# Modulation matmuls spread in twos over two stretches of a factorization, and a third token tile kept in SBUF

## The chip, the cores and the metric

The kernel runs on one NeuronCore of a Trainium2 chip. The metric is the device time of one launch in microseconds (us); lower is better. The engines that matter here are TensorE (PE, with its weight loads shown as PEld), VectorE (DVE), ScalarE (ACT), GpSimd (POOL) and SyncE (SP), which here only issues DMAs.

## The reference

The input `x` has 8 batches of 512 tokens of width 576, and `cond` one row of 576 per batch. Everything is float32.

```
# L0: a rotation in a 64-dimensional subspace
U, _ = qr(P)                                  # P: 576 x 64
A    = skew(silu(cond) @ W.T + b)             # 8 matrices of 64 x 64
R    = expm(A)
x    = x + ((x @ U) @ R - x @ U) @ U.T

# L1: a transformer block with modulation
shift1, scale1, gate1, shift2, scale2, gate2 = split(silu(cond) @ ada_w + ada_b, 6)
h = layernorm(x) * (1 + scale1) + shift1
q, k, v = h @ qkv_w + qkv_b                   # 16 heads of width 36
att = softmax(q . k over the 16 heads of the same token) @ v
x = x + gate1 * (att reshaped @ proj_w + proj_b)
h = layernorm(x) * (1 + scale2) + shift2
x = x + gate2 * (gelu(h @ fc1_w + fc1_b) @ fc2_w + fc2_b)
```

The attention is over the 16 heads of one token, so it is elementwise work and runs on DVE, one tile of 128 tokens at a time.

## The kernel before

**Preparation.** The kernel factors `P` first, column by column, in a loop of 64 steps (`qr_step(j, ...)`, L259). A step has two matmuls, `rp` (L262, it broadcasts the pivot row) and `dp` (L270, it sums the column products), two small activations on ACT (`nrm` L286 and `nsg` L287) and about 20 DVE instructions. They wait for each other in a ring. `rp` needs the updated `m` of the step before (L325). `dp` needs the column products `t` (L251 and L256), which DVE makes after that update. DVE's first instruction of a step (`sg`, L279) needs `rp`, and its `w` (L308) needs `nrm`, which needs `dp`. The steps get shorter as the columns that remain get fewer.

**Work beside the factorization.** TensorE has free time in each step, and the generator `beside()` (L508) fills it. After the instructions of step `j`, for `j` above 1, the loop calls `next(side, None)` once, and the generator issues one portion. In the order of the steps the portions are:

- steps 4 to 13: four matmuls of `skew_entries` each (L385), which make the entries of the skew matrices;
- steps 14 to 17: modulation, that is `modulations()` (L497). It has 9 groups of 384 columns. A group is five matmuls of 8 x 384 (`ada`, L352, one for each block of 128 rows of `ada_w`), and a copy of the sums to `ada_rows` on ACT (L354). After groups 1, 2, 5 and 7 comes one more unit, `modulation(v)`: five matmuls of 8 columns (`mod`, L363) and two activations on ACT (L369 or L371). Each matmul of `ada` and each `modulation` is one unit of the generator, 49 units in all. A group whose buffer is free again loads another (`load_ada`);
- steps 18 to 30: the series of `expm` (L425), with products of 64 x 64 matrices (L409) on TensorE, copies on ACT and sums on POOL. Where the series yields `True`, which it does in 12 of these 13 steps, a portion of the modulation is issued too;
- steps 31 to 49: the 19 squarings of `expm` (`pe` and `pf`, L409), without modulation;
- from step 50: what is left of the modulation.

A portion of the modulation is three units: `paced(3, [modulations()])` (L513) yields after every third. After the 12 units of steps 14 to 17 and 36 units of the series, one unit is left for step 50. When the last `ada` matmul is done, the SBUF of the preparation is given to the weights of the main part, so SP's loads that follow (L1004, L902, L970) wait for it.

All engines but SP run the instructions here in the order in which they are recorded (`tc.manual_schedule`).

**The first tiles.** After the factorization the kernel solves for the projection and begins the main part (L1106 on). A unit is one pair of token tiles of 128. `qkv(b, i)` (L787) multiplies one tile by `wqkv` in six groups of 288 columns (`qkvp`, L800), each summed in one of two PSUM buffers (`ps_mm`). ACT copies a group out. For the first two tiles of batch 0 (`stay`, L791) the copy goes straight to `tok`, one of three SBUF buffers with the tag `qkv` (L808). For any other tile the copy goes to `qs` (L811), ACT issues a DMA of it to `tok_d` in DRAM (L812), and `attention` loads the whole tile back later with a DMA from SP (L826). The attention of a unit reads it on DVE (L838, L845, L866, L873).

Between the pieces of attention of unit 0 the hand-written order places the rotations of batches 0 and 1 (`zps` L730, `rot` L741, the sum and the normalization L749 and L137 to L141, with one power on POOL, L140), the transposes `htr` (L773), and `next_sums` (L996): on POOL four tensor operations (L1007 to L1010) on weights of fc2, and the DMA of their result to `comb_d` (L1000).

The DMAs of all queues share eight completion semaphores in turn. A DMA is only issued when the DMA recorded eight places before it, on the same semaphore, has landed. A queue stands still while it waits for that.

**The main part.** From about 410 us the 16 units follow each other: projection, MLP on TensorE, and the attention of the unit after next beside it on DVE. It is the same before and after.

Of the kernel before, what the change touches and what calls it, by code (L numbers as in the profile page):

```python
# [48 lines left out]
def rotate_then_dit_block(  # L49
# [53 lines left out]
    def srows(c):  # L103
        return 65 if c == 4 else 128
# [47 lines left out]
    with tc.manual_schedule(engines=engines), tc.tile_pool(name="prep", bufs=1) as prep, tc.tile_pool(name="qrs", bufs=2) as qrs, tc.tile_pool(  # L152
# [177 lines left out]
        def paced(n, parts):  # L330

            k = 0
            for part in parts:
                for _ in part:
                    k += 1
                    if k % n == 0:
                        yield
# [6 lines left out]
        def load_ada(g):  # L344
            aws[g] = adap.tile([128, NK, AC], F32, tag="aw", name=f"aw_{g}")
            load_rows(aws[g], ada_w[:, g * AC : (g + 1) * AC], 65)

        def ada_columns(g):
            ps = ps_m.tile([B, AC], F32, tag="m", name=f"ada_{g}")
            for c in range(NK):  # L350
                k = srows(c)
                nc.tensor.matmul(ps, lhsT=sc[0:k, c, :], rhs=aws[g][0:k, c, :], start=c == 0, stop=c == NK - 1)  # L352
                yield
            nc.scalar.copy(ada_rows[:, g * AC : (g + 1) * AC], ps)  # L354
            for k in range(2):
                if g == (4, 8)[k]:
                    nc.sync.dma_start(out=gates_d[k], in_=ada_rows[:, (3 * k + 2) * D : (3 * k + 3) * D])

        def modulation(v):
            ps = ps_m.tile([128, NK, B], F32, tag="m", name=f"mod_{v}")  # L360
            for c, rows in enumerate(KROWS):
                first = v * D + c * 128
                nc.tensor.matmul(  # L363
                    ps[0:rows, c], lhsT=ada_rows[:, first : first + rows], rhs=ident[0:B, 0:B], start=True, stop=True
                )
            for c0, c1, rows in ((0, 4, 128), (4, 5, 64)):
                dst = mod[0:rows, v // 3 * 2 + v % 3, c0:c1, :]
                if v % 3:
                    nc.scalar.activation(dst, ps[0:rows, c0:c1], AF.Identity, bias=ones[0:rows, 0:1])  # L369
                else:  # L370
                    nc.scalar.copy(dst, ps[0:rows, c0:c1])  # L371
# [7 lines left out]
        def skew_entries(g):  # L379

            ps = ps_m.tile([B, GROUP], F32, tag="m", name=f"skew_{g}")
            cols = slice(g * GROUP, (g + 1) * GROUP)
            for c in range(NK):
                k = srows(c)
                nc.tensor.matmul(ps, lhsT=sc[0:k, c, :], rhs=wr[0:k, c, cols], start=c == 0, stop=c == NK - 1)  # L385
                yield
            nc.scalar.mul(skew[:, 1 + g * GROUP : 1 + (g + 1) * GROUP], ps, 2.0**-N_SQUARINGS)
# [3 lines left out]
        def skew_rows():  # L391

            nc.sync.dma_start(out=skew_d, in_=skew)
            for h in range(2):
                for k in range(2):
                    first = skew_d[h * 4 : h * 4 + 4, k * 32 : k * 32 + R]
                    src = bass.AP(tensor=first.tensor, offset=first.offset, ap=[[62, 32], [VD, 4], [1, R]])
                    nc.sync.dma_start(out=au[h * R + k * 32 : h * R + k * 32 + 32], in_=src)
# [98 lines left out]
        def modulations():  # L497

            for g in range(9):
                yield from ada_columns(g)  # L500
                if g + 4 < 9:
                    load_ada(g + 4)
                v = {1: 0, 2: 1, 5: 3, 7: 4}.get(g)
                if v is not None:
                    modulation(v)
                    yield

        def beside():  # L508
            yield
            yield  # L510
            yield from paced(4, [skew_entries(g) for g in range(8)])
            skew_rows()
            rest = paced(3, [modulations()])  # L513
            for _ in range(4):
                next(rest)
                yield
            for free in expm(*eyes):
                if free:
                    next(rest, None)
                yield  # L520
            for _ in rest:
                yield

        for g in range(4):
# [6 lines left out]
        first_xt = xin.tile([128, D], F32, tag="xt", name="xt_0_0", bufs=2)  # L531
        eyes = identities()
        side = beside()
        t, done = column_products(0), None
        for j in range(R):
# [251 lines left out]
    def qkv(b, i):  # L787


        hT = hTs[b]  # L790
        stay = b == 0 and i < 2  # L791
        if stay:
            tok = toks[b, i] = tiles.tile([128, 3 * D], F32, tag="qkv", name=f"qkv_{b}_{i}", bufs=3)

        def group(n):
            cols = slice(n * HALF, (n + 1) * HALF)
            ps = ps_mm.tile([128, HALF], F32, tag="mm", name=f"qkvp_{b}_{i}_{n}")
            for c in range(NK):
                k = srows(c)
                nc.tensor.matmul(  # L800
                    ps,
                    lhsT=hT[0:k, c, i * 128 : (i + 1) * 128],
                    rhs=wqkv[0:k, c, cols],
                    start=c == 0,
                    stop=c == NK - 1,
                )
            if stay:
                nc.scalar.copy(tok[:, cols], ps)  # L808
            else:
                qs = tiles.tile([128, HALF], F32, tag="qs", name=f"qs_{b}_{i}_{n}", bufs=4)  # L810
                nc.scalar.copy(qs, ps)  # L811
                nc.scalar.dma_start(out=tok_d[b][i * 128 : (i + 1) * 128, cols], in_=qs)  # L812

        return [lambda n=n: group(n) for n in range(6)]
# [294 lines left out]
    first[0]()  # L1109
    feature_major(0, 0)  # L1110
    q = qkv(0, 0)
    now(q[:2])
    first[2]()
    now(q[2:4])
    first[3]()
    next_sums()
    now(q[4:])
    q = qkv(0, 1)
    att = attention(*units[0])
    ops(4, att)  # L1120
# [6 lines left out]
    next_sums()  # L1127
    feature_major(0, 1)
    now(qkv(0, 2))
    ops(4, att)  # L1130
    next_sums()
# [129 lines left out]
```

## Time and profile before

| | |
|---|---|
| median of 3 runs | 2169.66 us (2166.77 to 2171.46) |
| profiled execution, its own time | 2173.5 us |
| its span, first to last instruction | 2171.8 us |
| PE busy in the span | 2074.7 us (96%) |
| DVE busy | 1825.2 us (84%) |
| ACT, POOL busy | 401.4 us (18%), 658.7 us (30%) |
| mean granted TensorE clock | 0.964 |

The profiled execution took 3.8 us longer than the median. Its span leaves out 1.7 us of its own time. Busy time is the union of the engine's instructions. The granted clock is the share of its full speed that TensorE was allowed; in this trace it is either 1.0 or 0.5 at any moment.

By stage, in the same trace, PE was busy for 157.7 of the 170 us from 240 to 410, and for 1634.1 of the 1650 us from 410 to 2060.

### The profile page before, as it was taken

The page shows a single profiled execution, that of the slowest core. Times are in us where ns is not written, and L with a number is a line of the kernel's source. Part 1 is how long each engine was busy: PE and PEld are TensorE (multiplying, and loading weights), DVE is VectorE, ACT ScalarE, POOL GpSimd, SP SyncE. Part 2 cuts the span into 40 slices and gives each one's busy share as a digit, 9 for nine tenths or more (in the row PEclk, how much of TensorE's full clock was granted, in tenths as well). Part 3 has the DMA queues.
Part 4 walks back from the last instruction along what each step waited for, and adds up shares of the span by engine and source line. Part 5 has one row for each costly group of instructions (what it writes and reads, how often), then busy time and mean ns, then how long its engine had stood idle before and what let it go on. Part 6 is the DMA issues. An engine that isn't in the chain of part 4 may idle for free.

```text
span 2171.8 us, 27934 instructions
## 1 busy us (share of the span) xinstructions
PE 2074.7 (96%) x10087; PEld 1676.4 (77%) x10087; DVE 1825.2 (84%) x2544; ACT 401.4 (18%) x896; POOL 658.7 (30%) x918
## 2 busy tenths in 40 slices
PE   5896998999999999999999999999999999999988
PEld 3475666887878788888878787878888887787867
DVE  8998499799997979879797979797997999996930
ACT  2232121212121211111121212121111111112110
POOL 2341143242323232323232232323232323233322
PEclk9955799999999999999999999999999999999999
DMA  8202265484939476665758494847666676676754
GB/s 276 87 2 75 85 213 160 135 238 156 271 125 266 158 229 200 191 197 185 237 146 269 126 276 129 267 157 229 198 176 229 196 223 181 193 207 198 220 154 123
DMA packets 239789, 400.79 MB, mean 185 GB/s; under 512 B 85502, under 2 KB 127435, under 8 KB 239652
## 3 DMA queue, kind: packets, MB, share of 16 engines
q1 hardware_dynamic: 213732, 372.46, 56.3%
q10 hardware_dynamic: 25920, 26.55, 3.6%
q8 instruction: 80, 1.31, 0.3%
q14 instruction: 57, 0.47, 0.1%
HBM read 340.01 MB, written 58.94 MB: 184 GB/s over the span
## 4 chain that ended last, share of the span: by engine, by line
PE 58%; DVE 24%; issue 10%; POOL 4%; DMA 2%; ACT 1%; ACTq 0%; SPq 0%; POOLq 0%; DVEq 0%
PE fc L973 24%; PE fc L1044 8%; PE fc L1049 5%; PE qkvp L800 5%; DVE sc L845 4%; DVE att L873 4%; DVE qk L838 3%; PE fc L1046 3%; DVE pv L866 3%; PE pj L928 2%; PE p L1059 2%; PE zps L730 1%; PE rot L741 1%; PE dp L270 1%; DVE m L325 1%
## 5 line engine op out<-in xcount | busy, mean ns | idle before, releaser
L973 PE MATMUL fc<-h2T,w 128*128 128x256 f32 (+1 forms) x2880 | 653.6, 381 | 2.3 <-ACT h2T L949 1.5
L973 PEld LDWEIGHTS fc<-h2T,w 128*128 128x128 f32 (+1 forms) x2880 | 539.8, 191 | 79.7 <-ACT h2T L949 8.8
L800 PE MATMUL qkvp<-wqkv,hT 128*128 128x288 f32 (+1 forms) x1920 | 485.0, 410 | 8.0 <-ACT qs L811 5.8
L800 PEld LDWEIGHTS qkvp<-wqkv,hT 128*128 128x128 f32 (+1 forms) x1920 | 364.2, 192 | 110.3 <-ACT qs L811 7.6
L838 DVE TENSOR_TENSOR qk<-qkv 128x2304 f32<-128x2304 f32 x128 | 336.7, 2630 | 18.8 <-DMA qkv<-tok 15.0
L866 DVE TENSOR_TENSOR pv<-sc,qkv 128x2304 f32<-128x2304 f32 x128 | 333.1, 2602 | 2.8
L873 DVE TENSOR_REDUCE att<-pv 128x144 f32<-128x2304 f32 x128 | 326.1, 2548 | 2.6
L845 DVE TENSOR_REDUCE sc<-qk 128x64 f32<-128x2304 f32 x128 | 326.2, 2549 | 2.4
L1029 POOL TENSOR_TENSOR ss<-gt 128x128 f32<-128x128 f32 x144 | 109.9, 763 | 643.9 <-ACT gt L981 643.9
L981 ACT ACTIVATE gt<-fc 128x512 f32<-128x512 f32 x144 | 86.0, 597 | 769.2 <-PE fc L973 739.9
L1049 PEld LDWEIGHTS fc<-wt,ss 128*128 128x128 f32 x1152 | 160.6, 190 | 15.1
L1049 PE MATMUL fc<-wt,ss 128*128 128x144 f32 x1152 | 164.7, 286 | 0.0
L1044 PE MATMUL fc<-wq,gt 128*128 128x288 f32 x576 | 163.2, 405 | 0.0
L811 ACT COPY qs<-qkvp 128x288 f32<-128x288 f32 x180 | 71.7, 398 | 412.1 <-PE qkvp L800 356.1
L989 POOL TENSOR_TENSOR x<-x,mt 128x288 f32<-128x288 f32 x64 | 71.1, 1111 | 211.5 <-DVE mt L988 211.5
L1044 PEld LDWEIGHTS fc<-wq,gt 128*128 128x128 f32 x576 | 107.6, 189 | 22.6
L1032 POOL TENSOR_TENSOR s<-gt 128x128 f32<-128x128 f32 x144 | 108.3, 752 | 0.0
L140 POOL TENSOR_TENSOR rstd_m<-rstd_m,mhalf 128x1 f32<-128x1 f32 x32 | 21.2, 663 | 279.3 <-DVE rstd_m L139 244.5
L928 PE MATMUL pj<-w2q_p,aT 128*128 128x288 f32 x384 | 104.8, 408 | 0.5 <-DVE u L1079 0.5
L1046 PE MATMUL fc<-wq,ss 128*128 128x288 f32 x288 | 93.9, 408 | 2.8 <-POOL ss L1031 2.6
L1044 PE MATMUL fc<-wt,gt 128*128 128x288 f32 x288 | 93.4, 406 | 0.0
L831 DVE COPY sc<-s 128x1 f32<-128x1 f32 x14 | 2.1, 153 | 104.0 <-POOL s L1032 104.0
(254 smaller groups left out, 2290.6 us busy)
## 6 DMA issues: line engine op xcount, KB each, us to landing
w<-in_fc_w SPq DMA_DIRECT2D x288, 320.0 KB
wq<-in_fc_q SPq DMA_DIRECT2D x144, 432.0 KB
wt<-comb_d SPq DMA_DIRECT2D x144, 432.0 KB
tok<-qs ACTq DMA_DIRECT2D x180, 144.0 KB
qkv<-tok SPq DMA_DIRECT2D x30, 864.0 KB
w2q_p<-in_proj_w SPq DMA_DIRECT2D x32, 432.0 KB
xT<-in_x_t SPq DMA_DIRECT2D x16, 640.0 KB
xt<-in_x SPq DMA_DIRECT2D x32, 288.0 KB
```

The costliest lines, as they stand in the source:

```text
L800: nc.tensor.matmul(ps, lhsT=hT[0:k, c, i * 128 : (i + 1) * 128], rhs=wqkv[0:k, c, cols], start=c == 0, stop=c == NK - 1,)
L838: nc.vector.tensor_tensor(pr, q[:, c * HC : (c + 1) * HC].unsqueeze(2).to_broadcast([128, HC, H, DH]), k.unsqueeze(1).to_broadcast([128, H ...
L845: nc.vector.tensor_reduce(sc[t][:, c * HC : (c + 1) * HC, :], pr, AX.X, ALU.add)
L866: nc.vector.tensor_tensor(pr, sc[t][:, c * HC : (c + 1) * HC, :].unsqueeze(2).to_broadcast([128, HC, DH, H]), v.unsqueeze(1).to_broadcast( ...
L873: nc.vector.tensor_reduce(att[:, c * HC : (c + 1) * HC, :], pr, AX.X, ALU.add)
L928: nc.tensor.matmul(ps, lhsT=aT[0:k, c, :], rhs=w, start=c == 0, stop=c == NK - 1)
L973: nc.tensor.matmul(ps[:, k], lhsT=w1[0:n, c, :], rhs=h2T[0:n, c, 0 : NU * 128], start=c == 0, stop=c == NK - 1,)
L1029: nc.gpsimd.tensor_tensor(ss[:, 0], gt[:, 0, 1], gt[:, 1, 1], ALU.add)
L1032: nc.gpsimd.tensor_tensor(s3s[g], gt[:, 0, 0], gt[:, 0, 1], ALU.subtract)
L1044: nc.tensor.matmul(p[k], lhsT=whole[k][0], rhs=whole[k][1], start=g == 0, stop=stop)
L1046: nc.tensor.matmul(p[2], lhsT=whole[2][0], rhs=whole[2][1], start=g == 0, stop=stop)
L1049: nc.tensor.matmul(bank[:, side], lhsT=lhs, rhs=rhs[:, n * QUARTER : (n + 1) * QUARTER], start=False, stop=stop, skip_group_check=True,)
```

## The change

There are two edits, in two stages that are far from each other.

The first is in `beside()`. The modulation is no longer paced in threes. `some(n)` takes `n` units of it. Steps 14 to 17 still take three each. The 12 steps of the series that issue modulation take two each, so that 24 units are issued there where there were 36. The 13 units that are left, where there was one, follow in steps 50 to 56: two in each, and one in step 56. The `modulation` unit after group 7 is among them, in step 53. The number of instructions is the same.

The second is in `qkv`: `stay` holds for `i < 3`. The third tile of batch 0 is copied straight to the third `qkv` buffer. Six DMAs that ACT issued (144 KB each) and one that SP issued (864 KB) are gone.

```diff
@@ beside()
             skew_rows()
-            rest = paced(3, [modulations()])
+            rest = modulations()
+
+            def some(n):
+                return [next(rest, ended) for _ in range(n)][-1] is not ended
+
+            ended = object()
             for _ in range(4):
-                next(rest)
+                some(3)
                 yield
             for free in expm(*eyes):
                 if free:
-                    next(rest, None)
+                    some(2)
                 yield
-            for _ in rest:
+            while some(2):
                 yield
@@ qkv(b, i)
         hT = hTs[b]
-        stay = b == 0 and i < 2
+        stay = b == 0 and i < 3
         if stay:
             tok = toks[b, i] = tiles.tile([128, 3 * D], F32, tag="qkv", name=f"qkv_{b}_{i}", bufs=3)
```

The order of the instructions on DVE and POOL is the same in both kernels. On PE only the modulation's matmuls move, within steps 18 to 56. On ACT the copies and activations of the modulation move with them, and six DMA issues go. On SP one load goes, and the last loads and stores of the modulation come with the units that they belong to.

## The prediction

> **What bounds the kernel now.** I read the page first, then the windows by stage, the waits of DVE, and the timelines of PE and ACT around the edits.
>
> ```profile
> span 2171.8 us, 27934 instructions
> PE 2074.7 (96%) x10087; PEld 1676.4 (77%) x10087; DVE 1825.2 (84%) x2544; ACT 401.4 (18%) x896; POOL 658.7 (30%) x918
> ```
>
> The page says PE, but that is the main part, which the change does not touch. Both edits lie ahead of 410 us, where stages follow each other without overlap: a microsecond saved or lost there arrives whole at the end. Up to 210 us the ring of the factorization sets the pace, so I ask what DVE waits for.
>
> ```profile
> DVE sg L279 <- PE rp L262: 3.1, 5, 1.1
> DVE w L308 <- ACT nrm L286: 0.9, 3, 0.3
> ...
> DVE w L308 <- ACT nrm L286: 2.5, 12, 0.2
> ```
>
> The first two lines are the waits of 50 to 125 us, the last of 175 to 210 us. Beside the series DVE stands still 3.1 us because `rp` came late, five times. DVE is busy otherwise, so this is nearly all that thinner portions can give there. In the last steps it loses 0.2 us a step to `nrm`.
>
> ```profile
> core 0: us, PE busy (x) PEld busy (x) DVE busy (x) ACT busy (x) POOL busy (x), PEclk, DMA share, GB/s
> 62.90:66.31 3.41, 2.88 (x12) 1.19 (x12) 3.28 (x21) 0.44 (x2) 0.00 (x0) 1.00 0.95 287
> 66.31:69.72 3.41, 3.31 (x18) 1.80 (x18) 3.36 (x18) 1.15 (x5) 0.72 (x1) 1.00 0.33 80
> 69.72:73.14 3.42, 3.32 (x7) 1.14 (x8) 3.08 (x20) 0.44 (x2) 0.00 (x0) 0.50 0.48 180
> 120.92:124.34 3.42, 1.87 (x36) 1.61 (x36) 3.33 (x18) 0.92 (x4) 1.03 (x2) 1.00 0.00 0
> 175.54:178.95 3.41, 3.36 (x15) 1.79 (x12) 3.14 (x19) 1.28 (x4) 0.61 (x1) 0.50 0.00 0
> ```
>
> The clock (PEclk) changes at the edges of windows of 3.41 us. A window of three `ada` a step (62.90) keeps it full. One with two `ada` and a `mod` (66.31) halves the next, though PE was busy 3.31 of 3.41 us. A window full of `ada` at half clock (69.72) restores it. So streamed columns count, not busy time, and two `ada` a step lie close to the edge.
>
> ```profile
> 63.31 2.10 PE L352 MATMUL ada<-aw,sc 128*8 128x384 f32 x6
> 70.38 3.45 PE L352 MATMUL ada<-aw,sc 128*8 128x384 f32 x6
> ...
> 176.70 1.45 PE L352 MATMUL ada<-aw,sc 65*8 65x384 f32 x2
> 178.15 0.60 PE L262 MATMUL rp<-m,ident 128*128 128x13 f32 x2
> 178.80 0.57 PE L270 MATMUL dp<-t,ones 128*128 128x13 f32 x2
> 180.69 0.60 PE L262 MATMUL rp<-m,ident 128*128 128x12 f32 x2 [1.32 <-DVE m L325]
> ```
>
> Three `ada` (six instructions) take 2.10 us at full clock, 0.70 each; at half clock 3.45, 1.15 each. In step 51 PE is free for 1.32 us, at half clock. One unit fits there, two do not.
>
> **Part 1a, steps 18 to 30: 12 units less.** With two units the late `rp` should go: after step 18 (3.45 us becomes 2.30, and DVE waited 0.6), 19, 28 (3.74 becomes 2.5; it waited 1.1), 29 and 30: −3.1 us. Against it, at full clock a step of two streams less, about as the window from 66.31 did, so the clock will halve more often. The trace has four half windows between 69 and 124 us (from 69.72, 97.03, 107.27 and 114.10). I expect one to three more. In one, a step with 64 x 64 products and two `ada` needs about 1.2 for `rp` and `dp`, 1.1 for products and 2.3, together 4.6 us, against some 3.5 us of DVE; half of that excess is hidden, since `rp` may come as late as DVE's `sg`. At some 0.45 us each, two windows give +0.9. Bounds: −4.0 (both waits, 3.1 and 0.9, gone) and +0.5 (eight such windows). I take −2.2, nearer the gain, because the five waits are rows of the trace and the extra windows are an estimate.
>
> The Trainium skill, "TensorE: Matmul & The Clock Gate", Part 1, says that the clock falls after an idle window of about 3.4 us and that gaps shorter than this keep it up. By that rule no step of twos would ever halve it, and 1a would be the whole −4.0. The row from 66.31 speaks against the rule: no idle gap, and the next window halved. I go by the row.
>
> **Part 1b, steps 50 to 56: 12 units more.** All of this lies on the ring. The clock is at half from 124.34 on, since squarings do not lift it. From `rp` to the portion is 1.00 us (175.70 to 176.70), so step 50 takes 1.00 + 2.4 = 3.4 us against 2.45: +0.9. A window of such steps is as full of `ada` as that from 69.72, so the clock should rise within step 51: +0.4. At full clock `rp`, `dp` and two units take 0.57 + 1.40 = 1.97 us, under DVE's 2.25, and the wait for `nrm` goes: −0.2 for step 52. Step 53 holds `ada`, the wait for ACT's copy (0.24 in the trace) and `mod` (1.26): 0.57 + 0.70 + 0.24 + 1.26 = 2.8 against 2.5 us, with its activations +0.4. As after 66.31 the next window is halved: +0.8 in steps 54 and 55. Steps 56 to 58 at full clock: −0.5. Sum +1.8. Bounds: −1.8 (full clock throughout, 0.25 us for each of 7 steps) and +6.9 (half clock throughout: five steps at +0.95, and step 53 at 4.6 against 2.5). The 175.54 row, with a single `ada`, stayed at half; two is where I count on the rise.
>
> ACT's copies (0.47 us) lie between two `nrm` as before. SP's loads for the main part, issued from 178.22 to 184.5 after the last `ada`, move about 15 us later. DMA is at 259 GB/s just after 178.95 and at 25 GB/s in 200 to 240, and their first user is `next_sums` behind 240: nothing. Were that cover gone, SP would be late by as much as the loads overlap 240 us, at most a few.
>
> **Part 2, the third tile.**
>
> ```profile
> 284.64 0.34 ACTq L812 DMA_DIRECT2D tok<-qs  x1
> 285.69 0.40 ACT L811 COPY qs<-qkvp 128x288 f32<-128x288 f32 x1 [1.47 <-PE qkvp L800]
> 290.06 0.34 ACTq L812 DMA_DIRECT2D tok<-qs  x1
> 290.44 0.40 ACT L811 COPY qs<-qkvp 128x288 f32<-128x288 f32 x1 [4.36 <-DMA comb_d<-tt]
> ...
> 290.89 5.12 PE L800 MATMUL qkvp<-wqkv,hT 128*128 128x288 f32 x20 [0.39 <-ACT qs L811]
> ```
>
> ACT's second store waits 4 us for a semaphore that a `comb_d` store holds, and the next copy behind it. But PE had two PSUM buffers and lost 0.39 us. That goes. The load back was issued at 298.73; the `xT` load queued behind it waits for PE's `zps` (done at 299.7) anyway, and DVE reads the tile first at 367.99, long after. From 250 to 365 us DVE is the bound; it idles 1.48 us for `rot` at 300.97, which comes earlier by the same 0.39 us. Stores recorded later get other neighbours on the eight semaphores, only for eight of them. The later stalls (ACT at 340 to 363 us) hang on POOL's `next_sums` and on DVE and stay. Bounds: −1.9 (0.39 and all of the 1.48) and +0.3 (a neighbour that lands late). I take −0.6.
>
> **Sum:** −2.2 + 1.8 − 0.6 = −1.0 us. The profiled execution of 2173.5 would be 2172.5; it lies 3.8 us above the median, so the median becomes 2169.66 − 1.0 = 2168.7 us. A difference under 0.2% (4.3 us) is about what a measurement of this kernel can't tell from none.
>
> **Rivals.**
> - *PE is never late.* The twos fit, the clock rises at once in step 50 and holds. Early −4.0, late −0.3, tile −0.6: −4.9 us, 2164.8 us. For it: the five waits are real, and 1.97 is under 2.25 us. Against: the 66.31 row.
> - *The round trip was on the path.* The chain of waits lists the stores and the load (2.1 and 4.4 us) between PE and POOL's power. If true, −6.5 us on its own: 2163.2 us. Against: that power (L140) reads only what DVE's L139 wrote, which ended at the same moment.
> - *Half clock in the last steps.* If two units a step don't lift the clock, 1b is +6.9; with −1.0 early and −0.6: +5.3 us, 2175.0 us. It decides if steps 50 to 55 take over 3.2 us each. For it: the clock stayed at half through 40 us of squarings with PE busy throughout, and in the 175.54 row. Against: the rise after 69.72.
>
> The change does what it says: the instruction order shows the units in steps 50 to 56 and seven DMAs less.
>
> **How the numbers follow.** Forecast 0.50, PE never late 0.22, round trip 0.08, half clock 0.20. Faster by over 0.2%: 0.30; same 0.50; slower 0.20. The range reaches from 2163.8 to 2174.0: it takes in the first rival and most of the bounds, and leaves out the two ends. The forecast's own range is 2165.4 to 2172.0.
>
> **What would show it.** `rp` waits of DVE in 50 to 125 us near zero, more half windows there; step 31 begins some 2 us earlier (before 118.67). Steps 50 and 54 over 3 us, 52 under 2.4 us, PEclk 1.00 in a window between 178 and 192 us. No 4 us stall of ACT near 286 us, and `rot` of the second batch 2 us earlier or less. Wrong, if steps 51 and 52 stay over 3.2 us, or if DVE's wait for `rp` stays at 3 us.

## The result, and the profile after

The changed kernel took 2176.61 us (median of 9 runs, 2173.73 to 2182.49) where the kernel before took 2171.70 us (median of 9 runs, 2166.77 to 2173.99). The ratio is 1.0029, with a 95% interval from 1.0017 to 1.0040. The forecast was 2168.7 us with a range up to 2174.0, so it was wrong, and on the slow side.

One comparison was not the whole of it. The same two kernels were compared twice more, with ratios 0.9998 [0.9984, 1.0011] and 1.0031 [1.0021, 1.0041]. Together the 30 runs of after have a mean of 2175.8 us, and 117 runs of before beside the experiments have 2172.1 us. So the change costs about 3.7 us, 0.17%. Single executions of either kernel scatter over some 15 us (before 2163.8 to 2179.3, after 2167.9 to 2182.8). Most of that scatter goes with the clock. Taking 2 x (1 - granted clock) x time as a run's time at half clock, each microsecond at half clock goes with 0.47 us of time in the 30 runs (correlation 0.93) and 0.49 in the 117 (0.90). The mean time at half clock is 169.0 us after and 155.8 before.

The profiled execution of after took 2179.26 us. Its page:

```profile
span 2177.5 us, 27915 instructions
...
PE 2088.9 (96%) x10087; PEld 1682.3 (77%) x10087; DVE 1825.0 (84%) x2544; ACT 401.4 (18%) x896; POOL 656.5 (30%) x918
```

The number of PE instructions is the same, and PE is busy 14.2 us longer: the same work at a lower clock. Next, what DVE waits for, from 50 to 125 us and then from 175 to 212 us of after (us in total, times, longest):

```profile
DVE sg L279 <- PE rp L262: 7.7, 7, 2.8
DVE w L308 <- ACT nrm L286: 2.1, 8, 0.3
```

```profile
DVE sg L279 <- PE rp L262: 1.8, 2, 0.9
DVE w L308 <- ACT nrm L286: 1.7, 8, 0.3
```

The wait for `rp` that should have gone to zero beside the series rose from 3.1 us to 7.7 (4.0 and 4.9 in the two later profiles of after), and 1.8 us came into the last steps, where there was none. The windows of 3.41 us show why (the window and its length; busy time and instructions of PE, PEld, DVE, ACT, POOL; granted clock; DMA share, GB/s):

```profile
71.86:75.27 3.41, 3.41 (x16) 1.56 (x16) 3.09 (x19) 0.51 (x4) 0.00 (x0) 0.50 0.25 90
75.27:78.68 3.41, 3.41 (x19) 1.01 (x16) 2.68 (x14) 0.53 (x2) 1.03 (x1) 0.50 0.02 5
...
95.75:99.16 3.41, 2.01 (x8) 0.81 (x8) 3.32 (x16) 0.44 (x2) 3.07 (x5) 1.00 0.00 0
99.16:102.58 3.42, 1.95 (x8) 0.63 (x7) 3.38 (x19) 0.91 (x3) 3.08 (x5) 1.00 0.08 15
102.58:105.99 3.41, 2.96 (x7) 1.37 (x8) 3.14 (x20) 0.44 (x2) 1.85 (x4) 0.50 0.75 250
...
181.08:184.50 3.42, 3.42 (x9) 1.22 (x8) 2.38 (x17) 0.33 (x2) 0.01 (x1) 0.50 0.02 5
184.50:187.91 3.41, 3.41 (x9) 1.13 (x8) 2.05 (x14) 0.80 (x3) 0.00 (x0) 0.50 0.00 0
187.91:191.32 3.41, 3.19 (x15) 1.32 (x14) 2.98 (x22) 1.04 (x5) 0.00 (x0) 1.00 0.00 0
```

From 71.86 us the clock is at half for five windows in a row, though PE does not pause at all in the first two. From 102.58 it is at half for 25 windows, past the end of the series. In the last steps the second of two windows of `ada` lifts it at 187.91, in step 52 (the forecast was within step 51). The costliest step at half clock is step 29, which took 6.01 us in all three profiles of after (before 4.19 and 3.85, with one `ada` more). On PE:

```profile
114.17 0.64 PE L262 MATMUL rp<-m,ident 128*128 128x35 f32 x2
114.62 0.62 PE L270 MATMUL dp<-t,ones 128*128 128x35 f32 x2
115.17 1.12 PE L409 MATMUL sn<-ex_lon,ex_a 64*64 64x64 f32 x16
116.23 0.59 PE L363 MATMUL mod<-ident,ada_rows 8*128 8x8 f32 x2
117.13 1.75 PE L363 MATMUL mod<-ident,ada_rows 8*128 8x8 f32 x8 [0.31 <-ACT ada_rows L354]
118.81 1.45 PE L352 MATMUL ada<-aw,sc 128*8 128x384 f32 x2
120.19 0.64 PE L262 MATMUL rp<-m,ident 128*128 128x34 f32 x2
```

and what DVE makes of it:

```profile
120.87 0.16 DVE L279 TENSOR_SCALAR sg<-rp 128x1 f32<-128x1 f32 x1 [2.82 <-PE rp L262]
```

From one `rp` to the next are 6.01 us, with PE at work nearly throughout. From one `sg` to the next are 6.01 us too, and of these DVE is busy 2.88 us and then waits 2.82 us.

The table has the stages of every profile, from the start of `rp` in one step to its start in another, and the time at half clock in two of them (us). The last column is the ratio of the runs to those of before.

| kernel | steps 14-17 | 18-30 | 31-49 | 50-62 | sum | half clock 14-30, 50-62 | ratio, 95% interval |
|---|---|---|---|---|---|---|---|
| before | 13.76 | 49.48 | 57.03 | 31.48 | 151.74 | 13.7, 31.5 | |
| before again | 13.75 | 49.48 | 57.03 | 31.44 | 151.70 | 13.7, 31.4 | 0.9999 [0.9985, 1.0014] |
| after | 13.75 | 53.40 | 56.02 | 32.97 | 156.14 | 38.3, 19.3 | 1.0029 [1.0017, 1.0040] |
| after again | 13.76 | 49.14 | 56.33 | 32.99 | 152.21 | 27.7, 19.3 | 0.9998 [0.9984, 1.0011] |
| after, third | 13.75 | 49.99 | 56.04 | 32.91 | 152.70 | 31.6, 19.3 | 1.0031 [1.0021, 1.0041] |
| tile only | 13.76 | 49.58 | 57.36 | 31.48 | 152.17 | 13.7, 31.5 | 0.9995 [0.9979, 1.0011] |
| twos only | 13.76 | 50.50 | 56.34 | 32.75 | 153.35 | 28.3, 19.1 | 1.0015 [0.9997, 1.0032] |
| late ones | 13.76 | 53.70 | 56.33 | 32.30 | 156.10 | 38.4, 32.3 | 1.0008 [0.9991, 1.0024] |
| threes, then none | 13.76 | 50.08 | 56.67 | 39.00 | 159.52 | 28.8, 39.0 | 1.0015 [1.0001, 1.0029] |
| filler | 13.75 | 53.11 | 56.89 | 32.83 | 156.58 | 17.1, 19.2 | 1.0021 [1.0008, 1.0034] |
| ones | 13.76 | 46.72 | 56.68 | 40.80 | 157.96 | 46.2, 30.6 | 1.0007 [0.9992, 1.0022] |
| modulation moved | 13.76 | 51.74 | 57.14 | 37.29 | 159.93 | 27.3, 33.9 | 1.0030 [1.0019, 1.0040] |
| spread | 17.11 | 45.18 | 56.70 | 32.30 | 151.30 | 45.0, 32.3 | 1.0004 [0.9994, 1.0014] |
| thin | 13.08 | 46.83 | 56.65 | 34.43 | 150.99 | 38.6, 34.4 | 0.9999 [0.9988, 1.0010] |

A ratio and the sum in its row need not agree: the sum is one execution, the ratio some ten, and the stages behind the factorization scatter as well (in the three profiles of after, the main part took 1784.9, 1781.5 and 1784.7 us, in the two of before 1784.6 and 1784.7). On average the three profiles of after have a sum 2.0 us above the two of before. So of the 3.7 us that the runs show, the stages of the modulation account for 2.0, and where the other 1.7 us lie is open.

### The profile page after: what moved, and what is told of

Same layout as the page of the kernel before. It is cut to its first block, busy times and chain, and to the rows that moved or that the text cites. A ratio compares the mean times of both kernels' runs of the same rounds, so it can differ in the third digit from the quotient of the medians.

```text
span 2177.5 us, 27915 instructions
## 1 busy us (share of the span) xinstructions
PE 2088.9 (96%) x10087; PEld 1682.3 (77%) x10087; DVE 1825.0 (84%) x2544; ACT 401.4 (18%) x896; POOL 656.5 (30%) x918
## 4 chain that ended last, share of the span: by engine, by line
PE 60%; DVE 23%; issue 9%; POOL 4%; DMA 2%; ACT 1%; SPq 0%; ACTq 0%; POOLq 0%; DVEq 0%
PE fc L978 24%; PE fc L1049 8%; PE qkvp L805 6%; PE fc L1054 5%; DVE sc L850 4%; DVE att L878 4%; DVE qk L843 3%; PE fc L1051 3%; DVE pv L871 3%; PE pj L933 2%; PE p L1064 2%; PE zps L735 1%; PE ada L352 1%; PE rot L746 1%; PE dp L270 1%
```

## The experiments

**The two edits apart.** First the tile without the modulation:

```diff
-        stay = b == 0 and i < 2
+        stay = b == 0 and i < 3
```

> The kernel before with the third tile kept on chip, and the modulation in threes as before. Theory A (the twos beside the series leave TensorE at half clock for stretches of several windows, and TensorE then sets the pace of the factorization) expects steps 14 to 63 to take 151.7 us as before (55.44 to 207.18), and the whole run within 1 us of before. Theory B (the tile costs: other neighbours on the eight semaphores delay a load of the main part) expects some 3 us or more slower than before, all of it after 240 us. My forecast's term for the tile was -0.6 us.

The factorization is that of before. The mechanism in the tile's stage is there too. DVE's wait for `rot` between 250 and 372 us, before and then with the tile alone:

```profile
DVE xt L749 <- PE rot L741: 1.6, 2, 1.5
```

```profile
DVE xt L749 <- PE rot L741: 0.9, 2, 0.7
```

and ACT's waits for the store of `comb_d` in the same stretch, before and with the tile alone:

```profile
ACT qs L811 <- DMA comb_d<-tt: 10.3, 2, 6.0
```

```profile
ACT qs L811 <- DMA comb_d<-tt: 6.0, 1, 6.0
```

ACT's stall of 4.4 us is gone and `rot` is 0.7 us earlier, but from the first `qk` of the attention to the main part it is 133.55 us against 133.71. What `rot` gained, something behind it gave back; the second profile of before has 133.53 us there, so the 0.16 us are no gain that these profiles can tell. Then the modulation without the tile, which is after's diff but for its last two lines:

> The changed kernel with only two tiles kept, that is the modulation's edit alone. Theory A expects the whole difference here: ratio to before 1.001 to 1.004, steps 14 to 31 some 2 to 5 us longer than before's 63.2 us, steps 50 to 63 some 1.5 us longer than 31.5 us, at least eight half-clock windows of 3.41 us between 69 and 124 us where before has four. Theory B expects it within 1 us of before.

Steps 18 to 30 are 1.0 us longer than before and not shorter, if less than the 2 to 5 us expected, with 28.3 us at half clock. That and the last steps (+1.3) is where the stages lose. The interval of this ratio takes in 1, but its 12 runs have a mean of 2175.7 us where the 30 of after have 2175.8. So as far as these runs can tell, the modulation's edit has the whole loss, and the tile neither gains nor loses anything that can be measured. The four experiments that follow keep two tiles as well.

**The last steps by ones.** To separate the last steps from the series:

```diff
-            while some(2):
+            while some(1):
```

> Twos beside the series, and the 13 units left one in each of steps 50 to 62, two tiles kept. Theory A expects the early loss of e2 again (steps 14 to 31 in 65 to 68 us) and less of the late one: one unit of 1.15 to 1.45 us fits in the 1.32 us that TensorE has free there at half clock, so steps 50 to 63 take 31.5 to 32.3 us and not 33. Theory C (the late units are what costs, and the early loss of the profiled run is chance of the clock's windows) expects the run within 1.5 us of before.

This is where "one unit fits, two do not" can be read. PE in steps 51 and 52:

```profile
182.03 0.60 PE L262 MATMUL rp<-m,ident 128*128 128x13 f32 x2
182.68 0.57 PE L270 MATMUL dp<-t,ones 128*128 128x13 f32 x2
183.18 1.45 PE L352 MATMUL ada<-aw,sc 65*8 65x384 f32 x2
184.57 0.60 PE L262 MATMUL rp<-m,ident 128*128 128x12 f32 x2
185.21 0.57 PE L270 MATMUL dp<-t,ones 128*128 128x12 f32 x2
185.71 1.45 PE L352 MATMUL ada<-aw,sc 128*8 128x384 f32 x2
```

All of this is at half clock. A step takes 2.54 and 2.52 us, the same as in before, where there was no `ada` in it: one a step costs nothing here. Nearly all of the 0.8 us more than before is the step with the `mod` (3.15 us against 2.41). And the early part, with the order of after, was 53.70 us. The ratio of 1.0008 can't tell this kernel from before.

**Where the units stand.** Threes as long as they last in the series (8 of its 12 portions), then none:

```diff
+            used = 0
             for free in expm(*eyes):
-                if free:
-                    some(2)
+                if free and used < 8:
+                    some(3)
+                    used += 1
                 yield
```

> The same 24 units beside the series and 13 in steps 50 to 56, but the 24 in threes in steps 18 to 25, and none in steps 26, 28, 29 and 30; two tiles kept. Theory A expects no early loss: as in the kernel before up to step 25, after it half clock with little work for TensorE, so steps 14 to 31 take 60 to 63 us, and steps 50 to 63 take 33 us, the run -2 to +2 us against before. Theory C expects it slower by as much as the changed kernel, 4 us or more.

Steps 18 to 30 took 50.08 us, 0.6 more than before, with 28.8 us at half clock; from step 14 on that is 63.8 us, 0.8 over the range expected. The surprise was the end: with the same twos in steps 50 to 56 as in after, steps 50 to 62 took 39.0 us and not 33, because the clock stayed at half:

```profile
180.19 0.58 PE L270 MATMUL dp<-t,ones 128*128 128x13 f32 x2
180.70 2.73 PE L352 MATMUL ada<-aw,sc 128*8 128x384 f32 x4
183.36 0.60 PE L262 MATMUL rp<-m,ident 128*128 128x12 f32 x2
183.81 0.58 PE L270 MATMUL dp<-t,ones 128*128 128x12 f32 x2
184.32 2.73 PE L352 MATMUL ada<-aw,sc 128*8 128x384 f32 x4
186.98 0.60 PE L262 MATMUL rp<-m,ident 128*128 128x11 f32 x2
187.43 0.58 PE L270 MATMUL dp<-t,ones 128*128 128x11 f32 x2
187.94 1.45 PE L352 MATMUL ada<-aw,sc 65*8 65x384 f32 x2
189.32 2.18 PE L363 MATMUL mod<-ident,ada_rows 8*128 8x8 f32 x10
```

Two `ada` take 2.73 us and the step 3.62. The window's edges here are at 182.73 and 186.15, and between them lie 0.63 us of the `ada` of step 51 and 1.83 of those of step 52, together 2.46. The window of after from 184.50 opened with the `ada` of step 51 and held all of them, 2.64 us up to `rp` at 187.14; the next was at full clock. The one before it, from 181.08, had 2.44 us and did not lift it. So in these steps it takes some 2.5 to 2.6 us of `ada` in a window, and two a step give that only where the edge falls well. Rows seem to count too: the fifth unit of a group streams over 65 rows, the others over 128. In after the window from 75.27 held 2.66 us of `ada`, 1.42 of them over 65 rows, and the next stayed at half; that from 85.51 held 2.66 us, all over 128 rows, and the next was at full clock. (The 2.44 us from 181.08 have 1.41 over 65 rows, the 2.46 us here none.) The figure is no rule for every window. Before, those from 97.03 and 114.10 lifted the clock with 2.4 us, and in the third profile of after that from 75.05 did so with 2.6 us, 1.4 of them over 65 rows. What lifted these is not shown. The rival "half clock in the last steps" happened here, at +7.5 us.

**A third stream that does nothing.** If too few streamed columns halve the clock, a useless matmul should hold it up:

```diff
                     some(2)
+                    nc.tensor.matmul(spare, lhsT=sc[:, 0, :], rhs=wr[:, 0, 0:AC], start=True, stop=True)
```

> Modulation as after, two tiles kept; each portion of the series is followed by one more matmul of an ada's shape (8x384 from 128 rows), whose sum nobody reads. So PE has three streams a step again in steps 18 to 30 and does more work than after, not less. Theory (two streams a step are too few to bring the clock back to full, and TensorE at half clock is the pacemaker): the half clock between step 14 and 31 falls from 38.3 us (after) to under 21 us (before: 13.7), steps 18 to 30 take 49 to 50.5 us (after 53.4, before 49.5), DVE's wait for rp there is 3 to 4 us (after 7.7). Rival (the new order itself, its ACT copies and mods at other steps, delays nrm and rp): steps 18 to 30 stay at 52 to 54 us or longer, since TensorE gets one matmul more a step. Both: steps 50 to 63 at 32.3 to 33.3 us.

Half right. The clock did what the theory says, 17.1 us at half against 27.7 to 38.4 with the same order and no filler; steps 18 to 27 took 35.1 us (before 36.1 and 37.7, the three profiles of after 39.3, 35.1 and 35.9). But step 27 has only products, the clock fell after it, and the third stream then made the late steps later:

```profile
110.44 0.64 PE L262 MATMUL rp<-m,ident 128*128 128x35 f32 x2
...
115.08 1.45 PE L352 MATMUL ada<-aw,sc 128*8 128x384 f32 x2
116.32 1.49 PE L526 MATMUL spare<-wr,sc 128*8 128x384 f32 x2
117.73 0.64 PE L262 MATMUL rp<-m,ident 128*128 128x34 f32 x2
```

Step 29 is 7.29 us, steps 28 to 30 together 18.0 (before 13.4 and 11.8), DVE's wait for `rp` is 7.8 us and not 3 to 4, and steps 18 to 30 take the rival's 53 us. Here more streams kept a full clock up to step 27; once it was half they were load and nothing else.

**One unit a step.** The opposite way, a series so thin that half clock does not matter:

```diff
                 if free:
-                    some(2)
+                    some(1)
```

> One unit a step in the 12 steps of the series, so 25 units are left for steps 50 to 62 in twos; two tiles kept. Theory (half clock makes TensorE late because two units do not fit beside the products at half clock): half clock nearly throughout from step 18 to 31 (40 us or more), but one unit fits, 1.2 + 1.1 + 1.15 = 3.45 us a step against some 3.5 of DVE, so DVE's wait for rp is under 2 us and steps 18 to 30 take 48 to 50.5 us. Rival (the thinner the portions, the longer): over 53 us with DVE's wait for rp over 6 us. Both: steps 50 to 63 at 32.5 to 35 us, the clock lifted within three steps of step 50; the whole 1 to 4 us slower than before by the first, over 5 us by the second.

DVE's waits in the series (68 to 116 us):

```profile
DVE w L308 <- ACT nrm L286: 2.3, 9, 0.3
DVE sg L279 <- PE rp L262: 1.5, 2, 1.3
```

The clock is at half nearly throughout (46.2 us) and steps 18 to 30 take 46.72 us, 2.8 less than before with its 13.7 us at half clock. It is the clearest verdict on the early part: where one unit stands in a step, half clock makes DVE wait no more than before. The gain itself is no shorter wait. In these steps DVE waits 1.5 us for `rp` and 2.3 for `nrm`, together 3.8 (before 2.7 and 0.9, together 3.6), but it is busy 42.07 us where it was 44.61, with the same instructions. Where such a difference can come from shows further down, with steps 31 to 49. The 25 units left over in twos then cost 9.3 us, since they stayed at half for six steps; I had expected 32.5 to 35 us.

**After and before once more.** 

> The changed kernel once more, unaltered, for the spread of its clock windows. If the half clock of steps 18 to 30 follows from the portions, it is 25 us or more again (38.3 in the first profile) and these steps take 50.5 us or more; if the first profile was an accident, under 20 us of half clock and 49 to 50 us. Steps 50 to 63 at 32 to 33.5 us, or near 39 if the clock is not lifted this time.

> The kernel before once more, unaltered, for the spread of its clock windows. If the first two profiles with this modulation are typical: half clock of 10 to 20 us in steps 14 to 30, steps 18 to 30 at 49 to 50 us, steps 50 to 63 at 31.3 to 31.7 us, all at half clock. If they were a lucky phase: over 25 us of half clock and over 51 us in steps 18 to 30.

Steps 18 to 30 of after took 49.14 us this time, with the same instructions in the same order that took 53.40 in the first profile; before gave 49.48 us twice. Where the edges of the clock windows fall among the steps differs from one execution to the next: the first edge after `rp` of step 18 came 1.42 us behind it in the first profile of after and 0.92 in the second. That this decides between 53.40 and 49.14 us fits, but no run sets the edge. The Trainium skill, "TensorE: Matmul & The Clock Gate", Part 1, says that the window runs freely and does not start anew with the kernel, which agrees. Threes ended up at the same place in the profiles of before, twos did not. A third comparison, with more runs:

> The changed kernel a third time, since its two medians against the kernel before disagree (1.0029 and 0.9998). If the clock windows of each execution decide and both comparisons drew from the same spread, the ratio lies between them, at 1.000 to 1.002, and steps 18 to 30 at 49 to 54 us with 25 to 40 us of half clock. If the kernel is truly 5 us slower, 1.002 or more again. Steps 26 to 30 take 20.5 to 21.5 us as in the four profiles with this order (before 19.7 and 17.6), steps 50 to 62 take 32.9 to 33.1 us.

The ratio was 1.0031, outside the 1.000 to 1.002 expected if chance alone had parted the first two. With all 30 runs the kernel is slower, and 0.9998 was the odd one: its 10 runs have a mean granted clock of 0.963, those of the other two 0.961 and 0.960. Why one group of runs fell better than the others stays open.

**The modulation out of step 29.**

```diff
-            for free in expm(*eyes):
+            for k, free in enumerate(expm(*eyes)):
                 if free:
-                    some(2)
+                    some(3 if k == 6 else 2)
```

> After, with three units in step 24, so that every later unit of the series comes one unit earlier and the modulation after group 5 falls into step 28, which has no products, and not into step 29 beside the product sn. One unit less is left for the last steps. If the meeting of sn, the modulation and half clock in step 29 costs what it seems to (6.01 us for the step, then 2.8 us of DVE's wait), step 29 falls to 3.5 to 4.8 us and steps 26 to 30 together to 18 to 20 us (after 21.0, before 19.7). If half clock alone is the cause, wherever the modulation stands, step 28 rises by as much as 29 falls and the five steps stay at 20.5 us or more. Half clock from step 26 on in both. Whole: 0 to 2 us faster than after.

Step 29 fell from 6.01 to 4.70 us and step 28 rose from 4.40 to 5.61: what left one came back in the other, as by the second reading. The five steps from 26 took 19.2 us and not 21, but steps 26, 27 and 30 were at full clock here. So no meeting of `sn` and `mod` as such; PE at half clock with more than it can do. The whole did not gain the 0 to 2 us expected (2178.2 us at the median, ratio 1.0030); in its last steps the clock stayed at half up to step 54.

**A version from these readings.** One `ada` is free beside a step at half clock, and also beside the skew entries. So the units go thinly everywhere, with the three tiles of after:

```diff
+            for k, _ in enumerate(paced(4, [skew_entries(g) for g in range(8)])):
+                if k > 0:
+                    some(1)
+                yield
...
-                    some(2)
+                    some(2 if k in (6, 7) else 1)
...
-            while some(2):
+            while some(1):
```

> The three tiles of after, and the 49 units thinly: one in each of steps 5 to 13 beside the skew entries (these nine in a PSUM bank of their own), three in steps 14 to 17, one in each step of the series but two in 24 and 25, one in each of steps 50 to 63. Theory (at half clock one ada fits beside the ring and two do not): steps 18 to 30 take 45.5 to 47.5 us (ones alone 46.7, before 49.5), steps 50 to 62 32 to 33 us (with ones there 32.3, before 31.5), steps 5 to 13 0 to 1.5 us longer than before; from step 14 to 63 it is 149 to 151 us against 151.7, and the whole 0 to 3 us faster than before. Rival (what is taken out of the series comes back elsewhere): steps 5 to 13 over 2 us longer or steps 31 to 49 back by as much, and the whole at 1.000 or above.

The series fell to 45.18 us (-4.3), a little under its range, and the last steps are at 32.30, as expected. DVE's busy time in the series, 41.56 us, is 3.0 of the 4.3. But two `mod` now stood in steps 14 and 16, the clock fell there, and these four steps rose by 3.35 us; and step 5 took 5.60 us, where it takes 4.50 in the next kernel, with no `ada` there. Steps 5 to 13 took 32.4 us, against 29.8 and 31.2 in the two profiles of before, so the rival's 2 us may have come true as well. The ratio is 1.0004. The last kernel mends both, with all `mod` at the end:

```diff
-                if k > 0:
+                if k > 1:
...
-                v = {1: 0, 2: 1, 5: 3, 7: 4}.get(g)
-                if v is not None:
-                    modulation(v)
-                    yield
+            for v in (0, 1, 3, 4):
+                modulation(v)
+                yield
...
-                    some(2 if k in (6, 7) else 1)
+                    some(2 if k in (0, 6, 7, 8) else 1)
```

> Like the spread version, with three edits: the early ones begin in step 6, not 5; the four modulation(v) units come last, after all 45 ada, so that steps 14 to 17 have three ada each and no mod; two ada in steps 18, 24, 25 and 26, one in the other steps of the series. Late: nine ada in steps 50 to 58, the four mods in 59 to 62. Theory (a step takes one ada at half clock for nothing; two, or a mod, cost 0.5 to 1 us; three ada a step hold the full clock): steps 6 to 13 as before within 0.5 us, 14 to 17 at 13.0 to 13.8 us (spread 17.1, before 13.8), 18 to 30 at 44.5 to 46.5 us (spread 45.2), 50 to 62 at 33.5 to 35 us since each mod costs some 0.7 us there; from step 14 to 63 147.5 to 150 us against 151.7, and the whole 1.5 to 4 us faster than before (0.998 to 0.9995). Rival (what leaves the series comes back): 14 to 63 at 151 us or more, the whole at 1.000 or above.

The sum is 150.99 us, 0.75 less than before, above the range of 147.5 to 150 and just under the rival's 151, and the whole is the same (2172.38 against 2172.89 us). The series is at 46.83, a little over its range, and the four `mod` cost 2.9 us at the end. No version here beats the kernel before by what can be measured. One thing did change: its 12 runs lie between 2171.14 and 2173.94, with a standard deviation of 1.0 us, where the 17 of before beside them have 3.4. In its profile the clock falls once, at 78.4 us, and stays down for 47 windows, so that no window's edge can change much; that the later stages scatter less too I can't explain.

## Why the prediction was wrong

**1a, steps 18 to 30 (forecast -2.2): the step that failed.** "I expect one to three more half windows" was the wrong term. There were 13.7 us at half clock before and 38.3, 27.7 and 31.6 in the three profiles of after: four to seven more windows. I saw that a window of two `ada` lies close to the edge, and counted single windows; I did not ask what brings the clock back. In the first profile of before, each half window held enough `ada` to be the last of its kind. With two `ada` and products a step, windows with PE busy 3.41 of 3.41 us stay at half, and the next ones with them: five in a row in the first profile of after, and from step 26 on 25 in all three.

The price was nearly right, but the gain was counted as if no half window would keep it. DVE's wait for `rp` in these steps was 2.7 and 3.7 us in the two profiles of before and 7.3, 3.6 and 4.5 in the three of after. Divided by the time at half clock, that is 0.67 and 0.92 us for each window of 3.41 us before, and 0.65, 0.44 and 0.49 after. The twos made a half window somewhat cheaper, and doubled or nearly tripled the number of them. So the -3.1 us did not come. Steps 19, 20 and 21 of the first profile, in one row of half windows, took 4.7 to 5.0 us and made DVE wait 1.3, 1.6 and 0.7 us. And step 29, which I had among the five that get shorter, took 6.01. The stage came to +3.9, -0.3 and +0.5 us. The bounds, -4.0 to +0.5, held one, touched another and missed the first by far; the value held none. Even the -0.3 is no success of the working: DVE's waits rose there too, by 1.7 us (`rp` 0.9, `nrm` 0.8), and its busy time fell by 1.8, from 44.61 to 42.79 us, for which I had no term.

The gain that I had counted on does exist: where the clock was full, steps 23 to 25 in all three profiles, no step with two `ada` kept DVE waiting for `rp`. With ones, at half clock, the wait for `rp` fell from 2.7 to 1.5 us; but `nrm` took that back, and that kernel's 2.8 us are nearly all DVE's busy time (2.5).

**Steps 31 to 49** had no term at all, and gave back 0.7 to 1.0 us. The clock is at half for 51.4 of the 57.0 us before and for all of the stage after, and DVE's waits for `rp` and `nrm` are 0.4 and 0.2 to 0.3 us in both. What fell is DVE's busy time, from 55.39 to 54.32, 54.52 and 54.32 us; in steps 31 to 34 it is 12.39 us in the first profile of before and 11.33 in each of after. DVE at the ends of steps 32 and 33 of before:

```profile
124.20 0.97 DVE L325 SCALAR_TENSOR_TENSOR m<-up,r,m 128x75 f32<-128x75 f32 x2
125.09 0.90 DVE L251 TENSOR_TENSOR pr<-m 128x75 f32<-128x75 f32 x2
...
128.16 0.50 DVE L325 SCALAR_TENSOR_TENSOR m<-up,r,m 128x75 f32<-128x75 f32 x2
128.57 0.38 DVE L251 TENSOR_TENSOR pr<-m 128x75 f32<-128x75 f32 x2
```

and POOL in the same stretch:

```profile
124.35 0.72 POOL L493 TENSOR_TENSOR ex_f<-ex_f,ex_i 128x256 f32<-128x256 f32 x1 [2.40 <-PE pe L409]
125.03 0.72 POOL L493 TENSOR_TENSOR ex_e<-ex_e,ex_i 128x256 f32<-128x256 f32 x1
129.19 0.72 POOL L493 TENSOR_TENSOR ex_e<-ex_e,ex_i 128x256 f32<-128x256 f32 x1 [3.44 <-PE pf L409]
```

Where POOL's two sums of a squaring ran, the same DVE work took 1.0 us longer, in steps 31 and 32 of before. In these steps of after no single `m` of L325 took over 0.30 us (before 0.80) and no `pr` over 0.24 (before 0.76); the sums fell on other instructions, which lost less. So when PE finishes a product also sets which DVE instructions POOL's sums slow down. How much of the difference in DVE's busy time in steps 18 to 30 comes the same way was not worked out.

**1b, the last steps (forecast +1.8): right in the sum, in part by luck.** It was +1.5, +1.5 and +1.4 us. Steps 50, 52 and 53 came close to the working (3.66 us for 3.4, 2.29 and 2.83 for 2.8). But step 51 cost 1.1 us and not 0.4, since the clock rose only in step 52, and steps 54 and 55 kept the full clock (1.97 and 2.38) and were 0.6 us shorter than before, not 0.8 longer; these errors nearly cancel. Nor is a window of twos "as full of `ada` as that from 69.72": that one held 2.8 us, the one from 181.08 2.44. The upper bound was real, too: with twos in these steps the clock was lifted only in step 55 in one other kernel and not at all in a second, at +5.8 and +7.5 us.

**The tile (forecast -0.6): right in mechanism, not in size.** ACT's stall went and `rot` came 0.7 us earlier, twice what I had counted. The stage shows -0.16 us with the tile alone, no more than the two profiles of before differ there, and the ratio of 0.9995 can't tell that from nothing.

**The rivals.** PE was late more than before, not never. The round trip was not on the path: no stage became shorter by anything near 6 us. "Half clock in the last steps" did not happen in after. It named the right cause in the wrong place: half clock that two units a step do not lift, but from step 18 on.

**The range.** It had the unknown of 1a at +0.5, for eight half windows more at 0.45 us each against a gain of 3.1. The first profile had seven more and cost 3.9. Besides, I took 2169.66 us, the median of three runs, as the base; 117 runs give 2172.1, so the range began 2.4 us too low.

## What to carry to other kernels

Filler work beside a chain does two things: it takes time in the step, and it holds the clock up. Thinned to two units here, it lost the second before it gained the first; so try a step either full enough to keep the clock or thin enough to fit at half clock, and look at what ends a half window before counting how many there will be. What leaves one stage also has to go somewhere: the thinnest kernel here was no faster as a whole. Compare the busy time of the engine in the ring as well as its waits. When a kernel's executions scatter by more than the effect, read the granted clock of every run, and profile the same kernel more than once before explaining a stage.

## What the runs showed of the hardware

PE busy without a pause did not restore the clock: two windows from 71.86 us were busy 3.41 of 3.41 us at half clock, and the next were still at half, while a window from 95.75 with PE busy 2.01 us was at full clock and the one after it too. The same part of the Trainium skill says that one busy window of about 3.4 us brings the full clock; these rows do not agree, and the rows decide. The products of 64 x 64 count for little: in steps 31 to 49 of after PE was busy 55.2 of 56.0 us, all of it at half clock. So does the `mod` of 8 columns: steps 14 to 17 were at full clock with three `ada` each in the last kernel, and the clock fell in the one before it, with a `mod` in place of an `ada` in two of them. `ada` of 384 columns counts for much, and seemingly more over 128 rows than over 65. And the same kernel, unaltered, took 49.14 or 53.40 us for the same 13 steps, with other places of the window edges among them. DVE's `m` and `pr` of a step took 0.97 and 0.90 us where POOL's sums ran beside them, and 0.50 and 0.38 where none did.
